# Row ends read from PSUM in their own iteration, and their other operations one per iteration ahead of S

## The chip, the cores and the metric

The kernel runs on one core of a Trainium2 chip. The metric is the time of one execution in device microseconds. The core's engines run side by side, each in its own order, and wait for one another through semaphores: TensorE (PE: matmuls, with the weight loads shown as PEld), VectorE (DVE), ScalarE (ACT), GpSimd (POOL) and SyncE (SP), which here only starts DMA transfers. Matmul results arrive in PSUM; everything else lives in SBUF.

## The reference

Four one-dimensional convolutions with 64 channels in and out and three taps run one after the other over 128 samples of length 1024. Their weights differ from sample to sample: a style vector scales the input channels, and each output channel is normalised. The second layer upsamples by two and blurs, the fourth blurs and downsamples by two. The input is added at the end.

```python
def _layer(x, style, w, b, mw, mb, typ):
    s = style @ mw.T + mb
    weight = SCALE * w * s[:, None, :, None]
    demod = lax.rsqrt(jnp.sum(weight * weight, axis=(2, 3)) + EPS)
    weight = weight * demod[:, :, None, None]
    if typ == 'same':
        out = vmap(_conv_same)(x, weight) + b[None, :, None]
    elif typ == 'upsample':
        out = vmap(_conv_up)(x, weight.transpose(0, 2, 1, 3)) + b[None, :, None]
        out = _blur(out, 2.0 * blur_k, (1, 1))
    elif typ == 'downsample':
        out = vmap(_conv_down)(_blur(x, blur_k, (2, 2)), weight) + b[None, :, None]
    return out
...
out = x
for i, typ in enumerate(('same', 'upsample', 'same', 'downsample')):
    out = _layer(out, cond_512, weights[i], biases[i], mod_w[i], mod_b[i], typ)
return x + out
```

## The kernel before, in words

Away from its ends a row passes through all four layers as one linear filter, because up- and downsampling cancel. So the kernel multiplies the four layers' weights into one set of nine taps per sample and applies that by a fast convolution. Only the three outputs at each end of a row need the four layers one by one; these row ends are computed for all 128 samples together.

The work is cut into 32 groups of four samples, one group per turn of the main loop. In turn `q` three groups are in flight: `n = q + 1`, `c = q + 2` and `s = q + 4`. The weights of a group are built in three stages, each of matmuls on PE and scaled copies on ACT:

- stage 1 (`stage1_a`, `stage1_b`) makes S for group `s`. In `stage1_b` DVE adds a last part from PSUM (L443), and POOL one more sum (L446).
- stage 2 (`stage2`, L468 or L534) makes R for group `c`; ACT copies it (L361), and DVE adds shared sums of it in `r_sums` (L589). In turns 5 to 27 part of stage 2 is shared: `share_sums` (DVE, L463), matmuls, and a copy on ACT (L491) into the bank that the next turn's stage 2 adds to. That bank shares its buffer with the one that L443 reads.
- stage 3 (`stage3_b`, `stage3_a`, L572) makes the taps Wf; DVE combines them into H in `combine_a` and `combine_b` (L660 and L663 with H).

The signal goes through input sums: G from X (`in_g2` and `in_g01`, DVE, L663 with G), and T from G and X (`in04` on DVE, L741; `in1`, `in2` and `in3` on POOL, L727, L732 and L712). Matmuls of T with H and Wf (L754, `conv0` to `conv4`) give products, which DVE adds up in `sum1` and `sum2` (L663 with y or Y, L813), and ACT scales into the output (L831). `copy_m3` is ACT's copy at L793.

The order on every engine is the order of the calls, written out by hand (`manual_schedule`); nothing is moved by a planner. Turns 0 to 3 are written in `early_turn`, 4 to 28 in `turn_of`, the last three in line.

Row ends take four matmul groups in PSUM banks Y: `ends0`, two parts of `ends1`, `ends2`; then `ends3` in a bank of its own. Before, `SLOTS` puts the first four at the end of turns 9, 12, 14 and 19, and `ends3` in turn 28. `slot` runs the matmuls and has ACT copy both banks into a tile `raw` (L854). DVE works on `raw` in SBUF, one or more turns later: `rest0`, `rest1` and `rest2` scale it and add a bias (L1015, L1016, L1040), `rest1_bias` adds biases (L1046, L1051), `blur_side` blurs (L1073). The table `EXTRA` says which of these, and which set-ups and parameters (`setup_x`, `setup0`, `setup1`, `setup3`, `var_newton`, `table_C`, `table_3`, `small_rest`, `zeros`), run in which turn. In `turn_of` all three entries of a turn are issued in a row: behind `sum1(n)`, and ahead of POOL's `in1` and `in2`. The next thing on DVE is the next turn's `r_sums`.

Some parameters of samples 32 to 127 (`REST`) are computed inside the loop. `small(q)` runs small matmuls into a spare stretch of a Y bank; `SMALL` names the turns, and `small_rest` takes up the result.

Of the kernel before, what the change touches and what calls it, by code (L numbers as in the profile page):

```python
# [48 lines left out]
F32 = mybir.dt.float32  # L49
AF = mybir.ActivationFunctionType  # L50
ALU = mybir.AluOpType
# [12 lines left out]
def kernel(  # L64
# [200 lines left out]
    def var_newton(bs, ls=slice(0, NL)):  # L265

        newton(var[:, ls, bs], dm[:, ls, bs], nw[:, ls, bs])
# [33 lines left out]
    def table_0(bs):  # L301
        table(nc_g, t0, bs, ALT, ODD, sc[:, 0, bs], 1.0)


    def table_C(bs, eng=nc_g):
        table(eng, tC, bs, slice(0, 2), slice(2, 4), dm[:, 1, bs], dm[:, 0, bs])

    def table_3(bs):
        table(nc_g, t3, bs, ALT, ODD, dm[:, 3, bs], var[:, 3, bs])
        table(nc_g, td, bs, slice(0, 2), slice(2, 4), dm[:, 3, bs], 1.0)  # L310

    def table_b(bs):
        table(nc_g, tb, bs, slice(0, 2), slice(2, 4), oc[:, bs], 1.0)
# [140 lines left out]
    def tap_differences():  # L454

        d = Ed[:, :4].rearrange("c (a b) o -> c a b o", a=2)
        for b in range(2):
            nc_g.tensor_sub(d[:, :, b], E[:, 4 * b : 4 * b + 5 : 4], E[:, 2:7:4])
        nc_g.tensor_sub(Ed[:, 4:], E[:, 3:8:4], E[:, 5:6].to_broadcast([P, 2, C]))
# [379 lines left out]
        )  # L839


    raw = [const.tile([P, 2, 512], F32, name=f"raw{i}") for i in range(2)]
    turn = [0]

    WIDE = 6

    def slot(matmuls, n, ps, wide=WIDE):

        matmuls(ps)
        turn[0] ^= 1  # L850
        r = raw[turn[0]]
        for i in range(2):
            src = ps[i][:, : HB * max(n, wide)].rearrange("c (b j) -> c b j", b=HB)
            nc_a.copy(r[:, i, : HB * n].rearrange("c (b j) -> c b j", b=HB), src[:, :, :n])  # L854

    def last(i, n, j):
        return raw[turn[0]][:, i, : n * j].rearrange("c (b j) -> c b j", j=j)


    a1, b1s, c0f, c2f, Da, oc = (  # L860
# [23 lines left out]
    def vector_Da(bs):  # L884
        nc_g.tensor_mul(Da[:, bs], sc[:, 3, bs], dm[:, 2, bs])
# [77 lines left out]
    def spread(t, n):  # L963

        return t[:, :, None].to_broadcast([P, t.shape[1], n])
# [7 lines left out]
    def setup_x(h):  # L973
        bs = slice(h * HB, (h + 1) * HB)
        nc_v.tensor_tensor(Xm[:, bs], Xe[:, bs], spread(sc[:, 0, bs], 8), op=ALU.mult)
# [35 lines left out]
            ps, 6, K, lambda i, r, c: wio[0][:, i, :], lambda i, r, c, m: Xs0[c][:, :, i : i + m]  # L1011
        )

    def scaled(dst, s, n, a, c):
        nc_v.tensor_tensor(dst, last(s, HB, n), spread(a, n), op=ALU.mult)  # L1015
        nc_v.tensor_tensor(dst, dst, spread(c, n), op=ALU.add)  # L1016

    def rest0(s):
        scaled(Ye[s][:, :, 1:7], s, 6, a0, c0)

    def ends1(part):

        n = 5 - part


        def weight(i, r, c):
            return g1[:, 2 * i + (part if c == 0 else 1 - part), :]

        def moving(i, r, c, m):
            col = 2 - i + (c + part if c else 0)  # L1030
            return Ye[c][:, :, col : col + m]

        return lambda ps: ends_matmul(ps, n, K, weight, moving)
# [8 lines left out]
    def rest1_bias(h):  # L1042

        bs = slice(h * HB, (h + 1) * HB)
        dst = Ue[h][:, :, 1:10]
        nc_v.scalar_tensor_tensor(  # L1046
            dst, spread(b1s[:, bs], 9), 2.0, dst, op0=ALU.mult, op1=ALU.add
        )
        for rows, col in ((T, 1), (Bo, 9)):
# [12 lines left out]
            lambda i, r, c, m: Ue[c][:, :, i + r : i + r + m],  # L1062
        )

    def rest2(s):
        scaled(Ve[s][:, :, 2:10], s, 8, a2, c2)


    def blur_side(s, part):
# [90 lines left out]

    stage2(0, None, BOTH, rest_of_scales)
    mod_matmul(LATER, pm[1][1], (2, 3))
    nc_a.copy(raw[0][:, 0, :n_later], pm[1][1][:, :n_later])
# [22 lines left out]
    const_rest(1, first, const_of(1, first))  # L1186
    in3(1)
    stage3(1, 0)
    mod_by_layer(LATER, raw[0][:, 0], sc, AF.Identity)
    conv1(0)  # L1190
    const_first(2, first)
    sum1(0)
# [7 lines left out]
    mod_by_layer(LATER, raw[0][:, 0], ssq, AF.Square)  # L1200
    scale3(3)
    conv2(0)


    REST = PART[2]
    SLOTS = {
        9: (ends0, 6),
        12: (ends1(0), 5),
        14: (ends1(1), 4),
        19: (ends2, 8),  # L1210
    }

    def high(n):
# [3 lines left out]
        1: (0, PART[1]),  # L1217
        2: (1, PART[1]),
        3: (2, PART[1]),
        5: (0, REST),  # L1220
        6: (1, REST),
        7: (2, REST),
    }

    def small(q):
# [8 lines left out]
    def small_rest(q):  # L1234
        l, bs = SMALL[q]
        const_rest(l, bs, high(bs.stop - bs.start))

    def layers(i, j):
        return REST, slice(i, j)
# [8 lines left out]
        (3, 2): lambda: (table_b(PART[1]), table_0(REST), vector_b1(REST), tap_differences()),  # L1248
# [21 lines left out]
        (29, 0): rest3_bias,  # L1270
    }

    def extra(*at):
        EXTRA.get(at, lambda: None)()

    AHEAD = 3
    FIRST = AHEAD + 1
# [108 lines left out]
    def turn_of(q):  # L1386
        n, c, s = q + 1, q + 2, q + 4
        entry = q == FIRST
        stage2(c)
        if entry:  # L1390
            sum2(q)
            conv4(q)
            r_sums(c)
        else:
            conv2(q)
            r_sums(c)
            sum2(q)
# [71 lines left out]
    conv3(n)  # L1469
    outputs(q, 2)  # L1470
    copy_m3(n)
    extra(q, 0)
    in04(n)
    in3(c)
    in_g01(c)
# [130 lines left out]
```

## Time and profile before

| What | us |
|---|---|
| median of 3 runs (lowest, highest) | 534.18 (530.38, 537.26) |
| the profiled execution | 530.83 |
| its span, first to last instruction | 529.0 |
| PE busy | 483.3 (91%) |
| DVE busy | 443.7 (84%) |
| ACT busy | 313.6 (59%) |
| POOL busy | 191.0 (36%) |
| mean granted clock of TensorE | 0.986 |

A row of the timeline has the start in us, the length in us, the engine, line and operation, output and inputs, their shape, the number of instructions merged, and in brackets how long the engine had been idle and what ended that. A row of the windows has a stretch, its length, the busy time of PE, PEld, DVE, ACT and POOL with instruction counts, the granted clock, the busy share of the DMA engines and GB/s. A row of the groups has the busy time, the mean ns of one instruction, and the idle time before them. A row of the waits has the total in us, the number and the longest.

### The profile page before, as it was taken

What the parts mean: (1) busy time and instruction counts of PE and PEld (TensorE: products, weight loads), DVE (VectorE), ACT (ScalarE), POOL (GpSimd) and SP (SyncE); (2) the same over time, 40 slices, a digit from 0 to 9 for tenths busy, and PEclk for the clock granted to TensorE, in tenths of its full rate; (3) what the DMA queues carried; (4) which work ended last, traced back from release to release, by engine and by line L of the source; (5) the groups of instructions that cost most, each with busy time, mean ns of one, the idle gap of its engine ahead of it and who ended that gap; (6) DMA issues with size and microseconds to landing.
All of it is one profiled execution on the core that took longest, in us unless ns stands there. A gap on an engine that the chain in (4) does not pass through costs nothing. (4 is left out here: it accounts for less than half of the span.)

```text
span 529.0 us, 26759 instructions
## 1 busy us (share of the span) xinstructions
PE 483.3 (91%) x11928; PEld 345.5 (65%) x11928; DVE 443.7 (84%) x691; ACT 313.6 (59%) x718; POOL 191.0 (36%) x198
## 2 busy tenths in 40 slices
PE   8999999987998888989899988998988898999876
PEld 7877888765776556756666655766555565676642
DVE  4799987799889888986969999759899989778694
ACT  5566666764666636656566755666655665665442
POOL 2442333245454234314444224444144422443300
PEclk9999999999999989989999999999899989999999
DMA  7217453443545333534444434453434443445224
GB/s 234 82 48 243 120 203 111 137 132 95 144 143 161 115 104 118 154 105 141 136 143 127 144 115 145 144 160 109 130 114 136 131 136 114 151 147 163 81 70 158
DMA packets 50498, 70.70 MB, mean 134 GB/s; under 512 B 5648, under 2 KB 47312, under 8 KB 50384
## 3 DMA queue, kind: packets, MB, share of 16 engines
q1 hardware_dynamic: 49792, 68.32, 41.7%
q8 instruction: 93, 1.52, 1.3%
q10 hardware_dynamic: 592, 0.69, 0.4%
q14 instruction: 21, 0.17, 0.1%
HBM read 35.36 MB, written 33.62 MB: 130 GB/s over the span
## 5 line engine op out<-in xcount | busy, mean ns | idle before, releaser
L754 PE MATMUL psA<-T,H 64*64 64x340 f32 x2304 | 185.4, 447 | 11.0 <-DVE H L663 7.9
L754 PEld LDWEIGHTS psA<-T,H 64*64 64x64 f32 x2304 | 86.8, 133 | 62.1 <-POOL T L712 7.7
L446 POOL TENSOR_TENSOR S<-S 128x128 f32<-128x128 f32 x28 | 19.6, 701 | 200.8 <-ACT S L361 200.8
L663 DVE SCALAR_TENSOR_TENSOR G<-X 128x1376 f32<-128x1376 f32 (+2 forms) x65 | 78.2, 1207 | 0.2
L754 PE MATMUL Y<-T,Wf 64*64 64x340 f32 x768 | 68.5, 488 | 7.8 <-DVE Y L663 7.7
L727 POOL TENSOR_TENSOR T<-G 128x684 f32<-128x684 f32 x28 | 46.5, 1661 | 70.7 <-DVE G L663 54.4
L754 PE MATMUL psA<-T,Wf 64*64 64x340 f32 x768 | 63.5, 446 | 0.0
L361 ACT ACTIVATE psW<-psA 128x128 f32<-128x128 f32 x100 | 19.3, 268 | 71.9 <-PE psA L572 67.6
L361 ACT ACTIVATE R<-psR,tC 128x448 f32<-128x448 f32 x63 | 36.6, 631 | 40.8 <-PE psR L468 23.5
L361 ACT ACTIVATE Wf<-psW,t 128x256 f32<-128x256 f32 (+2 forms) x76 | 32.8, 481 | 43.5 <-PE psW L572 43.2
L732 POOL TENSOR_TENSOR T<-G 128x684 f32<-128x684 f32 x28 | 52.2, 1863 | 0.0
L754 PEld LDWEIGHTS Y<-T,Wf 64*64 64x64 f32 x768 | 30.2, 141 | 31.7 <-DVE Y L663 12.5
L741 DVE TENSOR_TENSOR T<-G 128x1368 f32<-128x1368 f32 (+1 forms) x33 | 50.7, 1538 | 0.0
L712 POOL TENSOR_TENSOR T<-X 128x684 f32<-128x684 f32 x25 | 46.0, 1842 | 0.0
L468 PE MATMUL psR<-S,E 64*64 64x64 f32 (+1 forms) x1472 | 45.7, 237 | 0.0
L589 DVE TENSOR_TENSOR R<-R 128x256 f32<-128x256 f32 x25 | 27.7, 1107 | 21.4 <-ACT R L361 21.4
L390 PEld LDWEIGHTS psS<-wd,w2n 64*64 64x64 f32 x1120 | 33.8, 133 | 14.8 <-ACT S L361 0.8
L468 PEld LDWEIGHTS psR<-S,E 64*64 64x64 f32 x1472 | 38.1, 134 | 5.5
L831 ACT ACTIVATE o<-psA,tb,td 128x340 f32<-128x340 f32 x63 | 37.2, 649 | 6.2 <-PE psA L754 6.2
L663 DVE SCALAR_TENSOR_TENSOR y<-psA,m 128x680 f32<-128x680 f32 x32 | 27.7, 866 | 14.0 <-PE psA L754 7.7
L831 ACT ACTIVATE o<-Y,tb,td 128x340 f32<-128x340 f32 x63 | 36.7, 639 | 4.6 <-PE Y L754 2.7
L831 ACT ACTIVATE o<-y,tb,td 128x340 f32<-128x340 f32 x62 | 38.6, 679 | 0.6 <-DVE y L813 0.6
(166 smaller groups left out, 888.9 us busy)
## 6 DMA issues: line engine op xcount, KB each, us to landing
out<-o SPq DMA_DIRECT2D x167, 170.0 KB, 2.6
X<-in_x SPq DMA_DIRECT2D x150, 172.0 KB, 3.3
X<-in_x SPq DMA_DIRECT2D x14, 516.0 KB, 5.3
out<-o SPq DMA_DIRECT2D x6, 510.0 KB, 6.0
out<-o SPq DMA_DIRECT2D x2, 340.0 KB, 2.7
Xe<-in_x_ends SPq DMA_DIRECT2D x1, 512.0 KB, 6.5
out<-o ACTq DMA_DIRECT2D x3, 170.0 KB, 2.2
par<-in_params SPq DMA_DIRECT2D x2, 192.0 KB, 3.3
```

What stands on the lines that cost most here:

```text
L361: nc_a.activation(dst, src, AF.Copy, scale=f)
L390: nc.tensor.matmul(ps[r][cols, at * C : (at + n) * C], weight[rows], wd[c if r == 0 else 1 - c][rows, taps], start=first, stop=last, skip_ ...
L446: nc_g.tensor_add(t[:, :, 2], t[:, :, 2], t[:, :, 0])
L468: nc.tensor.matmul(dst[r][cols], weight[rows], st[c if r == 0 else 1 - c][rows, slots, :], start=False, stop=last, skip_group_check=True,)
L589: nc_v.tensor_add(t[:, :, 7:9], t[:, :, 2:6:3], t[:, :, 3:7:3])
L663: nc_v.scalar_tensor_tensor(out, x, f, y, op0=ALU.mult, op1=op)
L712: eng.tensor_sub(t[:, pairs, 0, :NJ], plane(X, 3, pairs), plane(X, 1, pairs))
L727: eng.tensor_add(t[:, :, 0, :NJ], plane(g, 2), plane(g, 1))
L732: eng.tensor_sub(t[:, :, 1, :NJ], plane(g, 2), plane(g, 1))
L741: nc_v.tensor_sub(t[:, pairs, :, :NJ], both(a, PL), both(b, 1))
L754: nc.tensor.matmul(ps[s][cols, :NB], w, Ts[q, tag][rows, c, i, g : g + NB], start=(g == 0 and m == 3), stop=(g == K - 1), skip_group_check ...
L831: nc_a.activation(dst, src, AF.Identity, bias=add, scale=d3)
```

## The change

- `slot` no longer copies to `raw`. It keeps the PSUM tile and its width, and `last` gives a view of it. The operation that reads the result follows in the same turn, directly behind the slot's matmuls and ahead of `sum1`. The turns of the slots become 10, 14, 15 and 19.
- `rest0` and `rest2` are split: the scaling reads PSUM in the slot's turn, and the addition (`add0`, `add2`) goes to the two turns behind it. `rest1_bias` is split into one wide operation per half and the four edges (`rest1_edges`).
- From turn 4 on `EXTRA` is gone. Two tables take its place: `TABLES` on POOL, issued behind `in3(n)`, and `SIDE`, issued behind `in_g2(c)` and so ahead of `stage1_b`'s DVE work on S; `in_g2` moves ahead of the memset. Where a turn had two halves of a thing before, `SIDE` mostly gives each half a turn of its own.
- The parameters of `REST` come sooner: `small` in turns 4 to 6 instead of 5 to 7; two Newton steps and `vector_c0` in turn 3; `table_C`, `vector_c2` and `vector_Da` in turn 4.
- In turn 28 `ends3` and `rest3` move behind the outputs, and `in_g01(c)` moves ahead of them, from behind `sum1`.

```diff
+    raw = const.tile([P, 512], F32, name="raw")
+    ends_ps = {}
     def slot(matmuls, n, ps, wide=WIDE):
         matmuls(ps)
-        turn[0] ^= 1
-        r = raw[turn[0]]
-        for i in range(2):
-            src = ps[i][:, : HB * max(n, wide)].rearrange("c (b j) -> c b j", b=HB)
-            nc_a.copy(r[:, i, : HB * n].rearrange("c (b j) -> c b j", b=HB), src[:, :, :n])
+        ends_ps[0] = ps, max(n, wide)
     def last(i, n, j):
-        return raw[turn[0]][:, i, : n * j].rearrange("c (b j) -> c b j", j=j)
+        ps, w = ends_ps[0]
+        return ps[i][:, : n * w].rearrange("c (b j) -> c b j", b=n)[:, :, :j]
...
     SLOTS = {
-        9: (ends0, 6),
-        12: (ends1(0), 5),
-        14: (ends1(1), 4),
-        19: (ends2, 8),
+        10: (ends0, 6, rest0),
+        14: (ends1(0), 5, lambda: rest1(0)),
+        15: (ends1(1), 4, lambda: rest1(1)),
+        19: (ends2, 8, rest2),
     }
...
-        (3, 0): lambda: var_newton(*layers(2, 3)),
+        (3, 0): lambda: (var_newton(*layers(2, 3)), var_newton(*layers(0, 2))),
...
-        (4, 0): lambda: var_newton(*layers(1, 2)),
-        (4, 2): lambda: vector_c0(REST),
-        (5, 0): lambda: (var_newton(*layers(0, 1)), var_newton(*layers(3, 4))),
-        (5, 2): lambda: (table_C(REST), small_rest(5), table_3(REST), vector_c2(REST), vector_Da(REST)),
-        (6, 1): lambda: small_rest(6),
-        (7, 1): lambda: small_rest(7),
-        (7, 2): lambda: (table_b(REST), zeros()),
-        (8, 0): lambda: (setup_x(0), setup_x(1)),
-        (9, 0): lambda: (setup0(), setup3()),
-        (9, 1): lambda: (setup1(0), setup1(1)),
-        (10, 0): lambda: rest0(0),
-        (11, 0): lambda: rest0(1),
-        (13, 0): lambda: rest1(0),
-        (15, 0): lambda: rest1(1),
-        (16, 0): lambda: rest1_bias(0),
-        (17, 0): lambda: rest1_bias(1),
-        (20, 0): lambda: rest2(0),
-        (21, 0): lambda: rest2(1),
-        (22, 0): lambda: (blur_side(0, 0), blur_side(1, 0)),
-        (23, 0): lambda: (blur_side(0, 1), blur_side(1, 1)),
-        (24, 0): lambda: (blur_side(0, 2), blur_side(1, 2)),
+    TABLES = {
+        4: lambda: (table_C(REST), vector_c2(REST), vector_Da(REST)),
+        5: lambda: table_3(REST),
+        6: zeros,
+    }
+    SIDE = {
+        4: lambda: var_newton(*layers(3, 4)),
+        5: lambda: small_rest(4),
+        6: lambda: small_rest(5),
+        7: lambda: (small_rest(6), table_b(REST)),
+        8: lambda: setup_x(0),
+        9: lambda: setup_x(1),
+        10: setup0,
+        11: lambda: add0(0),
+        12: lambda: add0(1),
+        13: lambda: (setup1(0), setup1(1)),
+        15: setup3,
+        16: lambda: rest1_bias(0),
+        17: lambda: rest1_bias(1),
+        18: lambda: (rest1_edges(0), rest1_edges(1)),
+        20: lambda: add2(0),
+        21: lambda: add2(1),
+        22: lambda: blur_side(0, 0),
+        23: lambda: blur_side(1, 0),
+        24: lambda: blur_side(0, 1),
+        25: lambda: blur_side(1, 1),
+        26: lambda: blur_side(0, 2),
+        27: lambda: blur_side(1, 2),
     }
...
             in3(n, eng=nc_g)
+        side(TABLES, q)
...
         if s < NQ:
             stage1_a(s)
-        else:
-            slot(ends3, 3, unit(ps_w, "psE"), 3)
...
+        in_g2(c)
+        side(SIDE, q)
         if q in SMALL:
             l, bs = SMALL[q]
             nc_v.memset(high(bs.stop - bs.start), 0.0)
-        in_g2(c)
...
         if s < NQ:
             stage1_b(s)
-            in_g01(c)
-        else:
-            rest3()
+        in_g01(c)
...
         if q in SLOTS:
-            slot(*SLOTS[q], Y_banks)
+            matmuls, width, rest = SLOTS[q]
+            slot(matmuls, width, Y_banks)
+            rest()
+        if s == NQ:
+            slot(ends3, 3, unit(ps_w, "psE"), 3)
+            rest3()
...
         sum1(n)
-        if s == NQ:
-            in_g01(c)
-        for i in range(3):
-            extra(q, i)
         in1(c, nc_g)
         in2(c, nc_g)
```

More of the change, by code (lines that the diff above doesn't have):

```diff
@@ L839, in store @@
         )
-    raw = [const.tile([P, 2, 512], F32, name=f"raw{i}") for i in range(2)]
-    turn = [0]
+    raw = const.tile([P, 512], F32, name="raw")
     WIDE = 6
+    ends_ps = {}
     def slot(matmuls, n, ps, wide=WIDE):
         matmuls(ps)
-        turn[0] ^= 1
-        r = raw[turn[0]]
-        for i in range(2):
-            src = ps[i][:, : HB * max(n, wide)].rearrange("c (b j) -> c b j", b=HB)
-            nc_a.copy(r[:, i, : HB * n].rearrange("c (b j) -> c b j", b=HB), src[:, :, :n])
+        ends_ps[0] = ps, max(n, wide)
     def last(i, n, j):
-        return raw[turn[0]][:, i, : n * j].rearrange("c (b j) -> c b j", j=j)
+        ps, w = ends_ps[0]
+        return ps[i][:, : n * w].rearrange("c (b j) -> c b j", b=n)[:, :, :j]
     a1, b1s, c0f, c2f, Da, oc = (
@@ L1012, in ends0, with rest0, add0 @@
         )
[L1014 to L1019, printed above, removed]
+    def rest0():
+        for s in range(2):
+            dst = Ye[s][:, :, 1:7]
+            nc_v.tensor_tensor(dst, last(s, HB, 6), spread(a0, 6), op=ALU.mult)
+    def add0(s):
+        dst = Ye[s][:, :, 1:7]
+        nc_v.tensor_tensor(dst, dst, spread(c0, 6), op=ALU.add)
     def ends1(part):
@@ L1048, in rest1_bias, with rest1_edges @@
         )
+    def rest1_edges(h):
+        bs = slice(h * HB, (h + 1) * HB)
         for rows, col in ((T, 1), (Bo, 9)):
@@ L1063, in ends2, with rest2, add2 @@
         )
-    def rest2(s):
-        scaled(Ve[s][:, :, 2:10], s, 8, a2, c2)
+    def rest2():
+        for s in range(2):
+            dst = Ve[s][:, :, 2:10]
+            nc_v.tensor_tensor(dst, last(s, HB, 8), spread(a2, 8), op=ALU.mult)
+    def add2(s):
+        dst = Ve[s][:, :, 2:10]
+        nc_v.tensor_tensor(dst, dst, spread(c2, 8), op=ALU.add)
     def blur_side(s, part):
@@ L1162 @@
     mod_matmul(LATER, pm[1][1], (2, 3))
-    nc_a.copy(raw[0][:, 0, :n_later], pm[1][1][:, :n_later])
+    nc_a.copy(raw[:, :n_later], pm[1][1][:, :n_later])
     for of in (vector_c0, vector_a1, vector_b1, table_3, vector_Da, vector_c2):
@@ L1188 @@
     stage3(1, 0)
-    mod_by_layer(LATER, raw[0][:, 0], sc, AF.Identity)
+    mod_by_layer(LATER, raw, sc, AF.Identity)
     conv1(0)
@@ L1199 @@
     stage3(1, 1)
-    mod_by_layer(LATER, raw[0][:, 0], ssq, AF.Square)
+    mod_by_layer(LATER, raw, ssq, AF.Square)
     scale3(3)
@@ L1219 @@
         3: (2, PART[1]),
-        5: (0, REST),
-        6: (1, REST),
-        7: (2, REST),
+        4: (0, REST),
+        5: (1, REST),
+        6: (2, REST),
     }
@@ L1245 @@
         (2, 2): lambda: (table_B(REST), table_Bn(REST), vector_a1(REST)),
-        (3, 0): lambda: var_newton(*layers(2, 3)),
+        (3, 0): lambda: (var_newton(*layers(2, 3)), var_newton(*layers(0, 2))),
         (3, 1): lambda: (table_A(REST, dm[:, 2, REST]), small_rest(3)),
-        (3, 2): lambda: (table_b(PART[1]), table_0(REST), vector_b1(REST), tap_differences()),
-        (4, 0): lambda: var_newton(*layers(1, 2)),
-        (4, 2): lambda: vector_c0(REST),
-        (5, 0): lambda: (var_newton(*layers(0, 1)), var_newton(*layers(3, 4))),
@@ L1263 @@
-        (16, 0): lambda: rest1_bias(0),
-        (17, 0): lambda: rest1_bias(1),
-        (20, 0): lambda: rest2(0),
-        (21, 0): lambda: rest2(1),
-        (22, 0): lambda: (blur_side(0, 0), blur_side(1, 0)),
-        (23, 0): lambda: (blur_side(0, 1), blur_side(1, 1)),
-        (24, 0): lambda: (blur_side(0, 2), blur_side(1, 2)),
-        (29, 0): rest3_bias,
+        (3, 2): lambda: (
+            table_b(PART[1]),
+            table_0(REST),
+            vector_b1(REST),
+            vector_c0(REST),
+            tap_differences(),
+        ),
+    }
@@ new lines @@
+    TABLES = {
+        4: lambda: (table_C(REST), vector_c2(REST), vector_Da(REST)),
+        5: lambda: table_3(REST),
+        6: zeros,
+    }
+    SIDE = {
[21 more added lines that the diff above has]
+        27: lambda: blur_side(1, 2),
@@ L1274, in extra, with side @@
         EXTRA.get(at, lambda: None)()
+    def side(work, q):
+        work.get(q, lambda: None)()
     AHEAD = 3
@@ L1471 @@
     copy_m3(n)
-    extra(q, 0)
+    rest3_bias()
     in04(n)
```

## The prediction

> **What bounds the kernel now.** I read the page first, then the waits of TensorE (PE), then equal turns of the main loop side by side, then the time order inside one bad and one good turn, then the clock.
>
> ```profile
> span 529.0 us, 26759 instructions
> PE 483.3 (91%) x11928; PEld 345.5 (65%) x11928; DVE 443.7 (84%) x691; ACT 313.6 (59%) x718; POOL 191.0 (36%) x198
> PEclk9999999999999989989999999999899989999999
> ...
> PE psA L572 <- DVE R L589: 19.4, 13, 1.9
> PE psA L754 <- DVE H L663: 7.9, 4, 3.2
> PE Y L754 <- DVE Y L663: 7.7, 15, 0.5
> ```
>
> PE is busy 91% of the span, and nearly all its idle time has three names, all on VectorE (DVE): the sum of R blocks (`r_sums`, L589), 13 waits, 19.4 us; the tap combinations H; and the Y sum that follows `r_sums`. The third column is the longest single wait. The clock row has four slices below 9.
>
> The windows below run from one `copy_m3` to the next, so each holds the end of one turn and the start of the next.
>
> ```profile
> 115.79:133.53 17.74, 14.59 (x396) 11.23 (x392) 16.35 (x28) 9.79 (x24) 9.01 (x12) 1.00 0.38 111
> 133.53:147.54 14.01, 14.01 (x396) 10.85 (x392) 12.06 (x24) 9.80 (x25) 6.22 (x4) 1.00 0.57 161
> ...
> 314.19:330.53 16.34, 14.21 (x392) 9.86 (x385) 15.51 (x22) 9.79 (x24) 6.15 (x4) 1.00 0.45 132
> 330.53:344.45 13.92, 13.92 (x392) 9.78 (x386) 10.95 (x19) 9.81 (x25) 5.81 (x4) 1.00 0.51 154
> 344.45:360.88 16.43, 16.43 (x416) 10.68 (x409) 10.81 (x19) 10.87 (x26) 5.61 (x4) 1.00 0.43 131
> ...
> 164.56:446.15 281.59, 255.08 (x6632) 174.32 (x6628) 244.96 (x346) 169.74 (x401) 103.31 (x68) 0.98 0.43 131
> 446.15:473.96 27.81, 27.81 (x776) 19.54 (x769) 21.88 (x37) 19.58 (x47) 11.62 (x8) 1.00 0.51 155
> ```
>
> Columns: window, length, busy time of PE, PEld, DVE, ACT, POOL, then clock and DMA. A turn without extra DVE work takes 13.92 us with PE busy throughout, and two in a row take 27.81 (DMA 155 GB/s, so transfers keep up at that pace). A turn behind an EXTRA entry takes 16.34, of which PE works 14.21; DVE then carries 15.5 us instead of 11.0. The 16.43 us turn holds the slot of `ends2`: 24 more matmuls, 2.5 us, PE never idle.
>
> Why the extra DVE work hurts is seen in time order. First the turn at 379 us, which runs `rest2(1)` (L1015, L1016) at the end of turn 21:
>
> ```profile
> 382.94 1.60 DVE L1015 TENSOR_TENSOR Ve<-raw,a 128x512 f32<-128x512 f32 x1
> 383.96 2.09 POOL L732 TENSOR_TENSOR T<-G 128x684 f32<-128x684 f32 x1
> 384.05 1.16 ACT L361 ACTIVATE R<-psR,tC 128x448 f32<-128x448 f32 x2 [0.83 <-PE psR L468]
> 384.58 2.02 DVE L1016 TENSOR_TENSOR Ve<-Ve,c 128x512 f32<-128x512 f32 x1
> 386.01 2.07 POOL L712 TENSOR_TENSOR T<-X 128x684 f32<-128x684 f32 x1
> 386.52 1.84 DVE L589 TENSOR_TENSOR R<-R 128x256 f32<-128x256 f32 x1
> 388.42 0.45 PE L572 MATMUL psA<-R,par 64*64 64x128 f32 x8 [1.65 <-DVE R L589]
> ```
>
> R is ready at 385.21, but DVE is inside L1016 until 386.60. Each DVE operation with both inputs in SBUF ends about 0.5 us (0.3 for the short L589) after the GpSimd (POOL) operation under way: L1016 at 386.60 after POOL's 386.05, L589 at 388.36 after 388.08. So the two engines exclude each other there, and the extra work lies exactly on POOL's stretch of `in1`, `in2`, `in3`. Now the good turn:
>
> ```profile
> 331.77 0.61 DVE L443 SCALAR_TENSOR_TENSOR S<-psS,tB,S 128x128 f32<-128x128 f32 x2 [0.62 <-PE psS L390]
> 332.27 0.66 ACT L491 COPY psR<-psA 128x256 f32<-128x256 f32 x2
> 333.54 0.40 PE L468 MATMUL psR<-S,E 64*64 64x128 f32 x8
> 333.87 0.87 DVE L663 SCALAR_TENSOR_TENSOR y<-psA,m 128x680 f32<-128x680 f32 x1
> 335.48 1.90 PE L754 MATMUL psA<-T,H 64*64 64x340 f32 x24
> 336.95 0.66 DVE L589 TENSOR_TENSOR R<-R 128x256 f32<-128x256 f32 x1 [2.21 <-ACT R L361]
> 337.26 1.85 POOL L712 TENSOR_TENSOR T<-X 128x684 f32<-128x684 f32 x1
> ...
> 340.24 0.56 DVE L663 SCALAR_TENSOR_TENSOR H<-H,Wf 128x384 f32<-128x384 f32 x1
> 341.17 1.90 PE L754 MATMUL psA<-T,H 64*64 64x340 f32 x24
> 344.63 0.75 POOL L446 TENSOR_TENSOR S<-S 128x128 f32<-128x128 f32 x1 [5.52 <-ACT S L361]
> ```
>
> Here DVE idles 2.21 us before L589 and 0.62 before S, and POOL is idle from 339.11 to 344.63; then it does L446, and waits again for the next `in_g01`.
>
> Last the clock, two pairs of adjacent windows:
>
> ```profile
> 367.82:371.23 3.41, 1.46 (x56) 1.07 (x48) 3.38 (x4) 0.18 (x2) 2.32 (x2) 1.00 0.05 10
> 371.23:374.64 3.41, 3.18 (x24) 1.52 (x28) 3.34 (x8) 1.44 (x6) 0.00 (x0) 0.50 0.67 205
> 401.95:405.36 3.41, 1.56 (x60) 1.26 (x52) 3.41 (x3) 0.00 (x0) 2.72 (x2) 1.00 0.02 6
> 405.36:408.78 3.42, 2.89 (x64) 1.90 (x64) 3.32 (x9) 1.62 (x6) 0.00 (x0) 1.00 0.71 202
> ```
>
> A stretch in which PE was busy 1.46 of 3.41 us is followed by 3.41 us at half clock; one with 1.56 is not. Half clock for 3.41 us costs 1.7 us. The low slices of the clock row are four such stretches.
>
> **The change part by part: what goes.** Against the profiled execution's own 530.83 us (span 529.0 and 1.8 around it; the median of the runs is 3.35 higher):
>
> 1. No EXTRA runs between `sum1` and `r_sums` any more in turns 4 to 28. Then L589 follows R as at 336.95, and its waits go: 19.4.
> 2. The Y sum stands right behind L589; 13 of its 15 waits of at most 0.53 go with it: 6.9.
> 3. PE's own busy time falls back from 14.21 to 13.92 in those 13 turns: 3.8.
> 4. The four half-clock stretches lose their cause: 4 x 1.7 = 6.8.
> 5. Waits for H. These come where POOL was late:
>
> ```profile
> 130.28 1.66 PE L754 MATMUL psA<-T,H 64*64 64x340 f32 x20 [3.15 <-DVE H L663]
> 161.31 1.95 PE L754 MATMUL psA<-T,H 64*64 64x340 f32 x24 [2.41 <-DVE H L663]
> 500.53 1.37 PE L754 MATMUL psA<-T,H 64*64 64x340 f32 x16 [1.40 <-DVE H L663]
> ```
>
> The first two follow tables and memsets that stood on POOL ahead of `in1`; they now stand behind `in3`, in POOL's 5.5 us pause, or go one turn sooner. The third follows an `in_g01` that stood behind `sum1` in turn 28 and now stands at its usual place. Together 7.0.
>
> The sum of what goes is 19.4 + 6.9 + 3.8 + 6.8 + 7.0 = 43.9 us. Cross-check of 1 to 4 by turns: 17 turns at 13.92 are 236.6, the four slots add about 7.3 (2.5 for `ends2` with 512 columns, as above; scaled from it, an estimated 1.9, 1.6 and 1.3 for 384, 320 and 256), together 243.9; the window of 281.59 is 37.7 longer, the terms give 36.9.
>
> **What is added or moved.** The DVE operations ahead of S now run behind `in_g2`, where POOL does at most L446. Their length there has no row, but
>
> ```profile
> L1016 DVE TENSOR_TENSOR Ve<-Ve,c 128x512 f32<-128x512 f32 x2 | 4.0, 2016 | 0.1
> L463 DVE TENSOR_TENSOR S<-S 128x256 f32<-128x256 f32 x23 | 9.6, 418 | 0.0
> L813 DVE TENSOR_TENSOR y<-y,psA 128x680 f32<-128x680 f32 x32 | 27.4, 856 | 0.0
> ```
>
> bound it: 2.0 us (the same operation under POOL) above, 0.42 (half as wide, POOL quiet) below. I take 0.7 for 512 columns, by L463 and L813, both without POOL's hold, plus up to 0.3 of L446's tail. Cover: 0.62 idle before S; then S may slip about 0.5 before the copy L491 reaches PE's stage 2 (L491 ends 332.93, PE starts 333.54), and `sum1` 0.7 before it reaches conv2 (334.74 against 335.48). So about 1.1 us is free; 1.0 costs nothing, 2.0 costs 0.9. Behind S stand `in_g01`, hence POOL's three operations, and `sum1`; POOL slipping by d holds the first H operation until 339.11 + d; H ends at 340.80 and PE takes it at 341.17, so PE waits from about d = 0.5. With d about 0.3 that is nothing. I book 0.1 for each of 17 turns: 1.7, between 0 and 15. Turn 13 is worse: four operations of `setup1`, 192 columns each, some 0.35 by L463, 1.4 us together against the 1.1, with H behind: 0.5. Turn 3 gets a second Newton step of three small operations on DVE, and turn 5 four table operations on POOL beside H: 0.5 each, between 0 and 1. Sum 3.2.
>
> The reads from PSUM in the slot turns wait for the slot's matmuls, two of about 0.7 (L813 reads PSUM at 680 columns in 0.86 while POOL works), and PE does a 1.9 us conv1 that `sum1` awaits anyway: nothing; uncovered, 1.4 in each of four turns. If they took L1015's 1.6 each, they would outlast conv1 and the 0.7 of slack by 0.6, 2.4 in all; reading PSUM faster than SBUF gains nothing, as the time is hidden. The ten ACT copies into `raw` go; ACT is busy 9.8 of 13.9: nothing. SP's list keeps its order and its DMAs; the slots merely move between turns. The memset's exchange with `in_g2`: nothing. In turn 28 `ends3` moves behind conv0 with the same matmuls: nothing.
>
> 530.83 - 43.9 + 3.2 = 490.1 us.
>
> **The rivals.**
> - *S becomes the new wait.* The operations ahead of it keep their 1.6 to 2.0 us; 0.5 to 0.9 stay uncovered in 18 turns, about 13 us, giving 503. For it: L446 lies just there. Against: POOL has no other work in that stretch.
> - *The half clock stays.* The four stretches might not come from the waits; then 490.1 + 6.8 = 496.9. Against: the one shown stands right behind a window in which PE was busy least. The Trainium skill (TensorE: Matmul & The Clock Gate, "What's actually happening") lets the clock fall after at least one idle window of about 3.4 us. No wait here exceeds 3.2 us, so by that rule the waits would not be the cause and the time would be this rival's. The trace disagrees with a strict reading: 43% busy was too little.
> - *Slower: POOL late in every turn.* If the work ahead of S takes so long that `in1` slips, H is held as at 130.28, where PE waited 3.15 and the turn took 17.74 instead of 14.01. Were that so in 18 turns, 3.7 x 18 = 67 would outweigh the 43.9: 554. It decides from about 2.8 us of slip (2.3 of wait a turn); the widest single operation would need more than its present 2.0. Against: POOL's pause.
> - *The change does not do what it says*: R itself (ACT) is the last releaser in 12 turns, and PE would wait there anyway: about 530. Against: the 27.81 us pair, where R releases and PE never waits.
>
> **How the numbers follow.** Forecast 490.1: 0.75 (its own range 485 to 496, the cost between 0 and 9). S as the wait, 503: 0.13. Half clock, 497: 0.05. No effect, 530: 0.03. Slower, 554: 0.04. The range 483 to 504 takes in the first three, with 2 us below the whole gain for a different execution. A measurement of this kernel tells about 2% (11 us): faster 0.93, same 0.03, slower 0.04.
>
> **What would show it.** Right: no wait of PE on L589 over 0.3 us in turns 8 to 27; L589 behind R with 2 us of DVE idle; turns of 14.0 us and slot turns of 15.5 to 16.5; operations such as L1016 and blur_side at 0.6 to 1.0 us; clock 1.00 throughout the loop. Wrong: PE waiting at stage 2 (psR) or conv2 (y) in turns with work ahead of S, H waits in most turns, or half-clock stretches without a wait in front.

## The result and the profile after

The changed kernel took 489.29 us (median; 487.75 to 491.01) against 532.74 us (530.38 to 537.26) for the kernel before, run beside it: a ratio of 0.918, 95% interval [0.910, 0.925]. The profiled execution took 488.37 us, its span 486.6. The prediction said 490.1 us, between 483 and 504.

First the head of the page and, from the waits, PE's rows that name DVE, with the row of DVE's own wait for R.

```profile
span 486.6 us, 26761 instructions
PE 472.5 (97%) x11928; PEld 343.2 (71%) x11928; DVE 396.2 (81%) x688; ACT 310.7 (64%) x708; POOL 186.6 (38%) x198
PEclk9999999999999999999999999999999999999999
...
PE psA L754 <- DVE y L663: 2.7, 2, 2.5
PE Y L754 <- DVE Y L663: 2.1, 5, 0.5
PE psA L572 <- DVE R L589: 0.5, 1, 0.5
DVE R L589 <- ACT R L361: 51.9, 25, 2.2
```

The span is 42.4 us shorter. PE's waits for `r_sums` (L589) fell from 19.4 us to 0.5, those for Y from 7.7 to 2.1, and the waits for H have left the list: 32.4 us together. PE's busy time fell by 10.8 us with the same 11928 matmuls. The clock row has no slice below 9 any more: a mean clock of 0.999 instead of 0.986 accounts for about 7 of it, an estimate; the rest is a faster pace of PE in turns without waits, whose cause no run isolates. The two make 43.2, so the account closes within 1 us. DVE carries 47.5 us less although it does almost the same work: that fits time in which it was held by POOL. In all 25 of its calls L589 now stands waiting for R (51.9 us), where before R was its last releaser in 12:

```profile
DVE R L589 <- ACT R L361: 21.4, 12, 2.2
```

Then the windows from one `copy_m3` to the next. Window k starts at the end of turn k-1, so the entry of turn k-1 in `SIDE` stands at its start, and its `r_sums` is turn k's.

```profile
114.58:130.06 15.48, 14.50 (x396) 11.08 (x392) 12.77 (x22) 9.79 (x25) 7.57 (x17) 1.00 0.47 142
130.06:144.11 14.05, 14.05 (x396) 10.91 (x392) 11.37 (x22) 9.78 (x24) 5.87 (x4) 1.00 0.54 153
...
229.97:244.85 14.88, 14.38 (x392) 10.52 (x386) 13.03 (x23) 9.86 (x24) 5.78 (x4) 1.00 0.51 149
...
304.32:318.98 14.66, 14.13 (x392) 10.56 (x386) 12.84 (x23) 9.87 (x25) 5.81 (x4) 1.00 0.47 143
318.98:335.42 16.44, 16.44 (x416) 10.68 (x410) 12.10 (x21) 9.79 (x25) 5.61 (x4) 1.00 0.44 135
335.42:349.49 14.07, 13.99 (x392) 9.78 (x386) 11.80 (x20) 9.94 (x25) 5.81 (x4) 1.00 0.53 153
...
158.11:405.84 247.73, 245.84 (x6632) 175.89 (x6628) 204.73 (x342) 167.41 (x393) 97.89 (x68) 1.00 0.49 148
```

A turn with a single operation ahead of S takes 14.0 to 14.1 us and PE hardly waits. The stretch of 17 turns that took 281.59 us takes 247.73, 17 times the 13.92 of a plain turn and 11.1 more: 8.0 in four slots, 1.7 in two turns that stand out, 14.88 behind `setup1` (turn 13) and 14.66 behind `rest1_edges` (turn 18), and 1.4 spread over the others. By the starts of `copy_m3` in both traces the 42.4 us come from here:

| windows | before | after | less |
|---|---|---|---|
| up to window 4 | 98.88 | 98.93 | -0.05 |
| 5 to 8 (last parameters) | 65.68 | 59.18 | 6.5 |
| 9 to 27 (row ends) | 309.40 | 275.77 | 33.6 |
| 28 and 29 | 28.63 | 26.73 | 1.9 |
| the rest | 26.41 | 25.99 | 0.4 |

Last the time order at 335 us, where `add2(0)` (L1074, the same addition as L1016 before) runs at its new place:

```profile
335.61 0.75 POOL L446 TENSOR_TENSOR S<-S 128x128 f32<-128x128 f32 x1 [8.25 <-ACT S L361]
335.96 0.95 DVE L1074 TENSOR_TENSOR Ve<-Ve,c 128x512 f32<-128x512 f32 x1
336.83 0.60 DVE L443 SCALAR_TENSOR_TENSOR S<-psS,tB,S 128x128 f32<-128x128 f32 x2
337.25 0.63 ACT L491 COPY psR<-psA 128x256 f32<-128x256 f32 x2
...
340.72 1.65 POOL L732 TENSOR_TENSOR T<-G 128x684 f32<-128x684 f32 x1
341.83 0.82 DVE L589 TENSOR_TENSOR R<-R 128x256 f32<-128x256 f32 x1 [2.13 <-ACT R L361]
342.33 1.82 POOL L712 TENSOR_TENSOR T<-X 128x684 f32<-128x684 f32 x1
```

The 2.02 us operation takes 0.95: it ends at 336.91, 0.55 behind the end of L446 (336.36), the same tail that the trace of before showed. DVE has no idle time ahead of S any more, but again 2.13 us ahead of L589.

### The profile page after: what moved, and what is told of

Read it like the earlier page. It is cut to its first block, busy times and chain, and to the rows that moved or that the text cites. A ratio compares the mean times of both kernels' runs of the same rounds, so it can differ in the third digit from the quotient of the medians.

```text
span 486.6 us, 26761 instructions
## 1 busy us (share of the span) xinstructions
PE 472.5 (97%) x11928; PEld 343.2 (71%) x11928; DVE 396.2 (81%) x688; ACT 310.7 (64%) x708; POOL 186.6 (38%) x198
## 5 line engine op out<-in xcount | busy, mean ns | idle before, releaser
L754 PE MATMUL psA<-T,H 64*64 64x340 f32 x2304 | 185.9, 447 | 2.9 <-DVE y L663 2.7
L754 PEld LDWEIGHTS psA<-T,H 64*64 64x64 f32 x2304 | 88.4, 133 | 52.4 <-DVE y L663 4.7
L446 POOL TENSOR_TENSOR S<-S 128x128 f32<-128x128 f32 x28 | 20.6, 735 | 162.4 <-ACT S L361 162.3
L663 DVE SCALAR_TENSOR_TENSOR G<-X 128x1376 f32<-128x1376 f32 (+2 forms) x65 | 78.0, 1205 | 0.2
L727 POOL TENSOR_TENSOR T<-G 128x684 f32<-128x684 f32 x28 | 46.5, 1659 | 74.4 <-DVE G L663 71.8
L754 PE MATMUL Y<-T,Wf 64*64 64x340 f32 x768 | 62.5, 452 | 3.0 <-DVE Y L663 2.1
L754 PE MATMUL psA<-T,Wf 64*64 64x340 f32 x768 | 63.5, 446 | 0.0
L589 DVE TENSOR_TENSOR R<-R 128x256 f32<-128x256 f32 x25 | 21.0, 839 | 51.9 <-ACT R L361 51.9
L361 ACT ACTIVATE psW<-psA 128x128 f32<-128x128 f32 x100 | 19.4, 268 | 49.6 <-PE psA L572 45.4
L732 POOL TENSOR_TENSOR T<-G 128x684 f32<-128x684 f32 x28 | 46.3, 1655 | 0.0
L754 PEld LDWEIGHTS Y<-T,Wf 64*64 64x64 f32 x768 | 28.7, 132 | 24.4 <-DVE Y L663 7.9
L712 POOL TENSOR_TENSOR T<-X 128x684 f32<-128x684 f32 x25 | 44.7, 1788 | 0.0
L390 PEld LDWEIGHTS psS<-wd,w2n 64*64 64x64 f32 x1120 | 34.1, 133 | 14.5 <-ACT S L361 0.8
L468 PEld LDWEIGHTS psR<-S,E 64*64 64x64 f32 x1472 | 39.6, 134 | 5.6 <-ACT psR L491 0.7
L754 PEld LDWEIGHTS psA<-T,Wf 64*64 64x64 f32 x768 | 28.3, 133 | 15.6
L663 DVE SCALAR_TENSOR_TENSOR Y<-m,psA 128x340 f32<-128x340 f32 x64 | 32.8, 512 | 7.7 <-PE psA L754 6.4
```

Source lines behind the costliest of these rows:

```text
L361: nc_a.activation(dst, src, AF.Copy, scale=f)
L390: nc.tensor.matmul(ps[r][cols, at * C : (at + n) * C], weight[rows], wd[c if r == 0 else 1 - c][rows, taps], start=first, stop=last, skip_ ...
L446: nc_g.tensor_add(t[:, :, 2], t[:, :, 2], t[:, :, 0])
L468: nc.tensor.matmul(dst[r][cols], weight[rows], st[c if r == 0 else 1 - c][rows, slots, :], start=False, stop=last, skip_group_check=True,)
L589: nc_v.tensor_add(t[:, :, 7:9], t[:, :, 2:6:3], t[:, :, 3:7:3])
L663: nc_v.scalar_tensor_tensor(out, x, f, y, op0=ALU.mult, op1=op)
```

## The experiments

The theory: the time went because DVE operations with two inputs in SBUF, placed between `sum1` and `r_sums`, were held by POOL's `in1` and `in2` and made R's sums late. All edits below are to the changed kernel unless another is named. Ratios are to the kernel before, run beside each.

**1. Is it the place, or POOL's hold?** Three kernels put extra operations of 512 columns into turns 8 to 27; `du` is a scratch tile that nothing reads.

```diff
+    du = const.tile([P, 2, 2, 256], F32, name="du")
+    def extra_work(src, n):
+        for i in range(n):
+            nc_v.tensor_tensor(du[:, 0], src, du[:, 1], op=ALU.add)
...
         sum1(n)
+        if 8 <= q < 28:
+            extra_work(du[:, 1], 2)        # pair_behind_sum1
+            extra_work(Y[:, :, :256], 2)   # pair_behind_sum1_psum, instead
...
         side(SIDE, q)
+        if 8 <= q < 28:
+            extra_work(du[:, 1], 1)        # one_more_ahead_of_S, instead
```

*pair_behind_sum1.* Expected: 

> The changed kernel with two extra additions of 512 columns on DVE, both inputs in SBUF, behind sum1 in each of turns 8 to 27; their result is used by nothing. Theory (an SBUF-SBUF operation there waits for POOL's running operation, so the pair ends behind R): PE again waits for r_sums and Y in these turns, about 2.3 us a turn, 46 us in all, and some half-clock stretches of 1.7 us come back, six or so: about 545 us (530 to 556). Rival (DVE has 2.1 us to spare there and the pair is 1.2 us of work): 489 to 494 us.

*pair_behind_sum1_psum.* Expected: 

> The same pair of 512 columns in the same place, but one input lies in PSUM; the result is used by nothing. Theory (only operations with both inputs in SBUF wait for POOL): each takes 0.7 us, 1.4 us fit into the 2.1 us that DVE idles, no wait of PE: 489 to 493 us. Rival (any work between sum1 and r_sums costs its turn 2.3 us, whatever its operands): about 535 us.

*one_more_ahead_of_S.* Expected: 

> The changed kernel with one extra addition of 512 columns on DVE, both inputs in SBUF, ahead of S in each of turns 8 to 27; its result is used by nothing. Theory (about 1.1 us is free there, and the changed kernel's single operations use nearly all of it): 0.6 to 0.9 us in each of the 16 turns without a slot, little in the four with one: about 500 us (496 to 506). Rival (there is ample room, since POOL is idle there): 489 to 492 us.

Measured, in this order: 542.74 us, ratio 1.014 [1.005, 1.022]; 489.39 us, 0.915 [0.909, 0.922]; 500.44 us, 0.936 [0.929, 0.944]. All three came as expected. For each kernel, the group of the extra operations and PE's waits tell why. The pair from SBUF behind `sum1`:

```profile
L848 DVE TENSOR_TENSOR du<-du 128x512 f32<-128x512 f32 x40 | 72.3, 1807 | 0.7
PE psA L572 <- DVE R L589: 29.3, 18, 2.3
PE Y L754 <- DVE Y L663: 10.5, 21, 0.5
```

The same pair with one input in PSUM:

```profile
L848 DVE TENSOR_TENSOR du<-Y,du 128x512 f32<-128x512 f32 x40 | 27.4, 684 | 0.7
PE psA L572 <- DVE R L589: 0.5, 1, 0.5
PE Y L754 <- DVE Y L663: 2.3, 6, 0.5
```

One more from SBUF ahead of S:

```profile
L848 DVE TENSOR_TENSOR du<-du 128x512 f32<-128x512 f32 x20 | 14.1, 707 | 0.0
PE Y L754 <- DVE Y L663: 9.4, 19, 0.5
```

The same shape takes 1.81 us beside POOL with both inputs in SBUF, 0.68 with one in PSUM, and 0.71 in SBUF where POOL is quiet. The pair from SBUF brings back the whole picture of the kernel before: waits for R and Y, and a mean clock of 0.972. From PSUM the identical place costs nothing. So it is POOL's hold and not the place as such. The third kernel is past the free room ahead of S: 14.65 us a turn instead of 14.05, 0.6 us for an operation of 0.71, and the wait that shows is at Y behind `r_sums`. The Trainium skill (SBUF — State Buffer, "Who interferes with whom") says that a DVE instruction with two SBUF inputs contends with a GpSimd instruction that reads SBUF, and one with at most one SBUF input, outside the 2-port performance modes, does not; 1807 against 684 ns agrees with it.

**2. Place against splitting.** In the kernel before, the entries of turns 8 to 27 are put ahead of S and nothing else is changed; in the changed kernel, its split entries of turns 8 to 27 except turn 10 are put back behind `sum1`.

```diff
(place_alone, in the kernel before)
         in_g2(c)
+        if 8 <= q < NQ - 4:
+            for i in range(3):
+                extra(q, i)
...
(side_behind_sum1)
         in_g2(c)
-        side(SIDE, q)
+        if q < 8 or q == 10:
+            side(SIDE, q)
...
         sum1(n)
+        if q >= 8 and q != 10:
+            side(SIDE, q)
```

*place_alone.* Expected: 

> The kernel before with one edit: in turns 8 to 27 the EXTRA entries run ahead of S instead of behind sum1, neither split nor spread, still on the SBUF copy of the row ends. Theory (the place, away from POOL's stretch, brings most of the gain, the spreading the rest): pairs of operations overrun the 1.1 us by about half a us, 0.6 to 0.8 a turn in a dozen turns, more in turn 9 with twelve operations; with the parameters and turn 28 as before, about 509 us (503 to 516). Rival (one operation a turn is what counts): 525 to 532 us.

*side_behind_sum1.* Expected: 

> The changed kernel with the work ahead of S put back behind sum1 in turns 8 to 27 (turn 10 excepted), still one operation or group a turn, still read from PSUM in the slot turns. Theory (a single operation ends with POOL's first one, ahead of R; the cost comes when two follow each other, or when POOL's later ones are pushed): some 0.5 us a turn for single operations, 2 to 4 us in turns 13, 15 and 18 with four operations: about 503 us (496 to 511). Rival (the place alone decides, number does not matter): 18 turns at 2.3 us and some half clock, about 531 us or more.

Measured: `place_alone` 504.7 us, ratio 0.948 [0.942, 0.953]; `side_behind_sum1` 497.5 us, 0.932 [0.925, 0.939]. With the place alone no wait on L589 is left in the list. PE's longest waits:

```profile
PE psA L754 <- DVE H L663: 8.2, 4, 3.1
PE Y L754 <- DVE Y L663: 5.7, 13, 0.5
```

The H waits are those of the old parameters and of turn 28, which this kernel keeps. In windows 9 to 27 it takes 280.95 us (309.40 before, 275.77 after): the place alone gives 28.4 of the 33.6. Its unsplit turns of 14.5 to 14.9 us pay what experiment 1 showed for too much ahead of S. The other kernel, with the old place, takes 285.08 us there, so what is left of the change gives 24.3, more than expected. That rest is splitting, spreading and the reads from PSUM together; no run separates the first two. One of its turns with four operations (`setup1`), and one with a single one:

```profile
230.54:246.92 16.38, 14.21 (x392) 9.86 (x387) 15.52 (x23) 9.79 (x24) 5.83 (x4) 1.00 0.44 135
...
341.76:356.12 14.36, 13.98 (x392) 9.78 (x387) 12.93 (x20) 9.88 (x24) 6.25 (x4) 1.00 0.49 143
```

```profile
345.88 1.62 DVE L1074 TENSOR_TENSOR Ve<-Ve,c 128x512 f32<-128x512 f32 x1
348.18 1.10 DVE L589 TENSOR_TENSOR R<-R 128x256 f32<-128x256 f32 x1 [0.67 <-ACT R L361]
```

In the time order of the second, a single held operation takes 1.62 us and still ends 0.67 us before R is there; the turn takes 14.36 us. Where more runs past R's arrival, it takes 16.38. Placing on the one hand, and splitting with the reads from PSUM on the other, are two remedies for one fault, and either takes most of it away.

**3. The reads from PSUM.** ACT's copies of the slot's result are put back, and the copy is read in the same turn.

```diff
     def slot(matmuls, n, ps, wide=WIDE):
         matmuls(ps)
-        ends_ps[0] = ps, max(n, wide)
+        w = max(n, wide)
+        for i in range(2):
+            nc_a.copy(raw2[:, i, : HB * w], ps[i][:, : HB * w])
+        ends_ps[0] = [raw2[:, 0], raw2[:, 1]], w
```

*raw_again.* Expected: 

> The changed kernel with ACT's two copies from PSUM put back into every slot; the row ends are then read from that SBUF copy in the same turn. Theory (reading PSUM matters only in that it does not wait for POOL; the slot turns cover what is lost): 0 to 2.4 us more than the changed kernel, about 490. Rival (the reads from PSUM carry the gain of the slot turns): 2.3 to 2.8 us in each of four turns, about 500 us.

Measured: 496.01 us, ratio 0.928 [0.924, 0.932]; the changed kernel beside it took 488.25 (`after_again`, below). The expectation missed, and the rival's price of 2.3 to 2.8 us a turn did not come either. In the profiled executions the span is 492.1 us against 486.6, and all of these 5.5 us lie in the four slot windows, 17.59, 17.14, 17.19 and 17.54 us against 15.96, 15.56, 15.69 and 16.44 (5.8 us). The time order in the first:

```profile
189.32 0.88 ACT L852 COPY raw<-Y 128x384 f32<-128x384 f32 x2
189.85 3.71 DVE L1017 TENSOR_TENSOR Ye<-raw,a 128x384 f32<-128x384 f32 x2 [0.44 <-ACT raw L852]
193.48 0.85 DVE L663 SCALAR_TENSOR_TENSOR y<-psA,m 128x680 f32<-128x680 f32 x1
194.39 1.95 PE L754 MATMUL psA<-T,H 64*64 64x340 f32 x24 [1.53 <-DVE y L663]
```

and in the changed kernel:

```profile
189.77 1.01 DVE L1013 TENSOR_TENSOR Ye<-Y,a 128x384 f32<-128x384 f32 x2
190.02 1.66 POOL L727 TENSOR_TENSOR T<-G 128x684 f32<-128x684 f32 x1 [2.83 <-DVE G L663]
191.52 0.87 DVE L663 SCALAR_TENSOR_TENSOR y<-psA,m 128x680 f32<-128x680 f32 x1 [0.74 <-PE psA L754]
```

From `raw` both inputs lie in SBUF while POOL runs L727 and L732, so two reads take 3.71 us, and `sum1` and conv2 wait: PE's waits for y rise from 2.7 us (2 waits) to 8.0 (6). From PSUM they take 1.01 beside that L727, and DVE is idle before `sum1`. In this place reading PSUM is worth 5.8 us: the hold of the reads and the copy ahead of them, which the run does not separate.

**4. Parameters and turn 28.** Each is put back as in the kernel before: `SMALL` in turns 5 to 7 with the old entries of `EXTRA`; `ends3` and `rest3` ahead of conv0, with `in_g01` behind `sum1`.

```diff
(parameters_undone)
-        4: (0, REST), 5: (1, REST), 6: (2, REST),
+        5: (0, REST), 6: (1, REST), 7: (2, REST),
...
(turn28_undone)
         if s < NQ:
             stage1_a(s)
+        else:
+            slot(ends3, 3, unit(ps_w, "psE"), 3)
...
         sum1(n)
+        if s == NQ:
+            in_g01(c)
```

*parameters_undone.* Expected: 

> The changed kernel with the last parameters as before: Newton steps, tables, memsets and small matmuls in the turns and places of the kernel before, up to turn 7. Theory (tables and memsets ahead of in1 make POOL late, and H waits): the four windows from turn 4 to turn 8 return from 59.2 to 65.7 us, about 495.8 us. Rival (these waits go with the rest): 489 to 491 us.

*turn28_undone.* Expected: 

> The changed kernel with turn 28 as before: ends3 ahead of copy_m3, in_g01 behind sum1. Theory: POOL's in1 is late again and PE waits 1.4 us for H in turn 29, 1.4 to 1.9 us more than the changed kernel, about 491 us. Rival (that wait has another cause): no difference.

Measured: `parameters_undone` 498.49 us, ratio 0.936 [0.930, 0.941], span 496.6; `turn28_undone` 491.46 us, 0.920 [0.916, 0.924]. In the first, three waits for H come back, the row `PE psA L754 <- DVE H L663: 6.8, 3, 3.1`, and windows 5 to 8 take 67.4 us instead of 59.2. They are the H waits of the kernel before without turn 28's, and a half-clock stretch in window 6 adds about 1.5 us; another follows in the tail, so the time lies above the expected 495.8. In the second, the H wait of 1.4 us returns and its window takes 15.61 us instead of 13.98, as expected. The medians lie further apart, 3.2 us beside `after_again`; in the profiled execution a half-clock stretch in the tail, at 470.97, adds about 1.7.

**5. The two turns that stand out.** `groups_in_slot_turns` puts `setup1` into turn 14 and the edges into turn 19, the slots' own turns. `groups_spread` puts `setup1` beside `setup0` in turn 10 and one half of the edges each into turns 18 and 19; `groups_spread_late` adds half of `setup3` to turn 5.

```diff
(groups_in_slot_turns)
-        13: lambda: (setup1(0), setup1(1)),
+        14: lambda: (setup1(0), setup1(1)),
-        18: lambda: (rest1_edges(0), rest1_edges(1)),
+        19: lambda: (rest1_edges(0), rest1_edges(1)),
(groups_spread)
-        10: setup0,
+        10: lambda: (setup0(), setup1(0), setup1(1)),
-        13: lambda: (setup1(0), setup1(1)),
-        18: lambda: (rest1_edges(0), rest1_edges(1)),
+        18: lambda: rest1_edges(0),
+        19: lambda: rest1_edges(1),
```

*groups_in_slot_turns.* Expected: 

> The changed kernel with setup1 in turn 14 instead of 13 and the edges of rest1 in turn 19 instead of 18, so that both groups of four operations run in turns with a slot, whose extra matmuls give PE work meanwhile. Theory: the windows of 14.9 and 14.7 us fall to 14.0, 1.5 us less than the changed kernel, about 487.8 us. Rival (the groups cost the same wherever they run): no difference.

*groups_spread.* Expected: 

> The changed kernel with setup1 in turn 10 beside setup0 (a turn with a slot whose matmuls need neither) and the edges of rest1 one half in turn 18, one in turn 19. Theory: the windows of 14.9 and 14.7 us fall to 13.9 and 14.1, that of turn 10 grows by 0.2 at most, that of turn 19 by 0.3, about 1 us less than the changed kernel, 487.3 us; a wait of PE's slot matmuls as when both groups stood in turns whose own matmuls need them should not come. Rival (any group of four costs its turn 0.7 to 0.9): no difference.

*groups_spread_late.* Expected: 

> The same, and the first two of setup3's four copies in turn 5 behind small_rest. Theory (in the window from 114.6 us r_sums comes just as POOL starts its third operation and waits 1.5 us for it; 0.4 us more work ahead of S makes POOL later, so that r_sums comes first): the window of 15.5 falls to about 14.5, 1 us less than the kernel beside it, about 486.4 us. Rival (more work ahead of S only adds): 0.4 us more.

*after_again*, the changed kernel once more beside the first of these. Expected: 

> The changed kernel itself, beside the next three on the same chip: 487 to 492 us.

Measured, in this order: 488.78 us, ratio 0.915 [0.912, 0.919]; 488.49 us, 0.916 [0.913, 0.920]; 488.38 us, 0.916 [0.912, 0.920]; and `after_again` 488.25 us, 0.915 [0.911, 0.918]. None differs from the changed kernel, so the gains expected of the first three did not come. In the first the two windows fell to 13.90 us each, but the slot windows rose from 15.56 to 16.70 and from 16.44 to 17.15: by the program the slot's matmuls need what was moved into their turn, a dependency that I had overlooked. The trace shows the wait in the first of the two slots; in the second it books no wait, only more time in PE's matmuls.

```profile
243.97 1.79 DVE L967 SCALAR_TENSOR_TENSOR g<-par,g 128x192 f32<-128x192 f32 x4
245.82 1.95 PE L995 MATMUL Y<-Ye,g 64*64 64x384 f32 x24 [0.91 <-DVE g L967]
```

In the second both windows fell (13.88 and 14.07) and the slots hardly moved (15.84 and 16.55), so windows 9 to 27 take 1.4 us less. But in the tail, where each of these kernels has a wait of 2.5 us for y, a half-clock stretch follows in the profiled execution:

```profile
461.77:465.18 3.41, 1.03 (x16) 0.30 (x8) 3.41 (x4) 1.16 (x2) 0.00 (x0) 1.00 0.53 181
465.18:468.59 3.41, 3.27 (x24) 1.54 (x28) 1.97 (x6) 0.00 (x0) 0.00 (x0) 0.50 0.06 23
```

In that of the changed kernel the border between two 3.41 us stretches of the clock cuts the wait in two, and no half clock follows:

```profile
462.07:465.48 3.41, 2.61 (x40) 1.11 (x30) 3.41 (x3) 1.79 (x4) 0.00 (x0) 1.00 0.48 163
465.48:468.89 3.41, 1.69 (x24) 1.00 (x28) 3.38 (x8) 0.42 (x1) 0.00 (x0) 1.00 0.29 102
```

It is not peculiar to `groups_spread`: in `after_again`, the changed kernel's own program, half clock follows in the tail from 466.58. At the same mean clock of 0.996 `after_again` took 489.8 to 489.9 us and `groups_spread` 488.1 to 489.2, which fits the 1.4 us, though on another chip.

In the third, window 6 stayed at 15.60 us where 14.5 was expected: R and POOL moved together, and L589 met the start of L712 as before. What would part them there stays open.

## Why the prediction held, point by point

*What goes (43.9 us).* Step 1 booked 19.4 for L589; 18.9 went. Step 2 booked 6.9 for Y; 5.6 went, and five short waits remain. Step 5 booked 7.0 for H; 7.9 went. Steps 3 and 4 (PE's pace and the half clock) booked 10.6; PE's busy time fell by 10.8. The sum of the measured parts is 43.2. Each is a difference of before and after and so already holds what the change added at that place; beside the span's 42.4 us stands the forecast's net of 43.9 - 3.2 = 40.7. Experiment 1 shows the cause of steps 1 to 4, since one edit brings all of them back (PE busy 491.9 us, 19.4 more than in the changed kernel, of which half clock at a mean of 0.972 makes about 15, an estimate); experiment 4 shows that of step 5.

*What is added (3.2 us).* The 0.1 a turn was right: the 14 windows from 8 to 27 without a slot or a group of operations lie 1.7 us in all above 13.92. The operation ahead of S took 0.95 us where 0.7 plus up to 0.3 of L446's tail was assumed, and its bare price was 0.71 (experiment 1). The slots were estimated at 1.9, 1.6, 1.3 and 2.5 us above a plain turn and took 2.04, 1.64, 1.77 and 2.52. Turn 13 was booked at 0.5 and took 0.96; turn 18's edges, four operations of 64 columns, were booked at 0.1 like a plain turn and took 0.74. The prediction priced columns, but so small an operation still takes 0.34 us on average, as the edges' group by form in the changed kernel shows (0.53 for the first, beside L446, and 0.27 to 0.28 for the others):

```profile
L1053 DVE SCALAR_TENSOR_TENSOR Ue<-b1s,Ue 64x64 f32<-64x64 f32 x4 | 1.4, 340 | 0.0
```

Turn 3's Newton step, booked at 0.5, cost nothing (windows 3 and 4: 32.38 us after, 32.32 before). Turn 5 was booked at 0.5 for table work beside H; a loss shows in turn 6 instead, at L589:

```profile
121.33 1.67 POOL L712 TENSOR_TENSOR T<-X 128x684 f32<-128x684 f32 x1
121.38 1.91 DVE L589 TENSOR_TENSOR R<-R 128x256 f32<-128x256 f32 x1 [2.23 <-ACT R L361]
```

L589 starts 0.05 us after L712, is held to its end and takes 1.91 us; PE then waits 0.5 us for it and 0.5 for the Y sum. At 341.83 L589 started with only 0.54 us of L732 left and took 0.82. These errors are below 1 us each and of both signs.

*Where S's slip goes.* The prediction said that a late S shows as waits at stage 2 (psR) or at conv2 (y), then at H. With too much ahead of S, PE waits for Y instead: 9.4 us in `one_more_ahead_of_S`. Of the chain only its order is in the rows: S, then `in_g01`, then POOL's operations, then an L589 that is held and a Y sum behind it. Turn 14 of the changed kernel, behind `setup1`, shows its end in small:

```profile
236.09 1.64 POOL L732 TENSOR_TENSOR T<-G 128x684 f32<-128x684 f32 x1
236.71 1.30 DVE L589 TENSOR_TENSOR R<-R 128x256 f32<-128x256 f32 x1 [1.61 <-ACT R L361]
239.04 1.95 PE L754 MATMUL Y<-T,Wf 64*64 64x340 f32 x24 [0.51 <-DVE Y L663]
```

*The step that failed.* The prediction held that "reading PSUM faster than SBUF gains nothing, as the time is hidden", with 2.4 us as the bound: `raw_again` measured 5.8. The bound left out ACT's copy ahead of the reads and took 1.6 us for each read, where each took 1.9 beside POOL. The forecast was not touched, because the change reads from PSUM.

*The rivals.* S as the new wait: 503 did not come, as the operations take 0.95 and not 1.6 to 2.0. The half clock went with the waits in the loop; one stretch in the tail comes and goes from run to run. POOL is not late in every turn; where the work ahead of S is doubled (`one_more_ahead_of_S`), the price is 0.6 us a turn, far from 3.7. That R itself would hold PE is refuted by 51.9 us of DVE waiting for R with PE busy 97%.

## What to carry to other kernels

A DVE operation with both inputs in SBUF should not stand beside a stream of GpSimd operations that read SBUF; if it must, one input left in PSUM took its price from 1.81 to 0.68 us here. What matters is not how much DVE does but whether it is free when the operand arrives that PE waits for, so one held operation ahead of it cost about 0.3 us a turn here (14.36 against 14.07) and two held ones 2.3 and more (16.4 to 18.2 in `pair_behind_sum1`). When moving small operations, count instructions as well as columns, and look at which matmul of the target turn reads their result.

## What the runs showed of the hardware

*Half clock.* In `pair_behind_sum1` two pairs of adjacent windows frame the border:

```profile
421.93:425.34 3.41, 1.57 (x56) 1.32 (x48) 3.41 (x3) 0.00 (x0) 3.09 (x2) 1.00 0.17 42
425.34:428.76 3.42, 2.87 (x56) 1.83 (x60) 3.35 (x8) 1.61 (x6) 0.00 (x0) 1.00 0.69 195
438.99:442.40 3.41, 1.56 (x57) 1.17 (x48) 3.38 (x4) 0.00 (x0) 2.59 (x2) 1.00 0.05 15
442.40:445.81 3.41, 2.92 (x24) 1.30 (x28) 3.34 (x8) 1.61 (x6) 0.00 (x0) 0.50 0.70 203
```

PE busy for 1.56 of 3.41 us was followed by half clock, 1.57 was not; the kernel before had 1.46 on the one side and 1.56 on the other. The border is not quite sharp: in `pair_behind_sum1` the stretch from 213.71, with 1.59, was followed by half clock. Laid over the traces that show the beat, from 20 us on, all stretches with 1.51 or less were followed by it and none with 1.65 or more. So here a stretch with about 1.9 us of idle PE or more costs up to 1.7 us in the next one. The stretches run at their own beat (193.74, 227.87, 371.23 and 422.43 in the kernel before are whole numbers of 3.41 us apart), so it depends on the phase whether one wait of 2.5 us is cut in two, as in the tails of experiment 5. The Trainium skill (TensorE: Matmul & The Clock Gate, "What's actually happening") has the clock fall after at least one idle window of about 3.4 us; here a window that was a little more than half idle was enough.

*Who comes first.* Of two operations that exclude each other, the later one waits for the end of the earlier: at 121.38 L589 waited for all of L712 and took 1.91 us, at 341.83 only for the rest of L732 and took 0.82. In both it ended 0.3 us behind POOL's operation. A shift of half a microsecond on one engine thus changes the length of L589 by 1.1 us.

*How long a held operation still takes.* Over all traces a held TENSOR_TENSOR operation ends, in the median, 0.28 us behind POOL's operation with 256 columns, 0.42 with 384 and 0.55 with 512: about 1.04 ns for each column. Unheld, the same widths took 0.42 (256) and 0.68 (512). So the hold puts off nearly the whole operation and hides only some 0.13 us of it, an estimate from these numbers.
